# A recurrent loop on one core: two gates share 128 PSUM columns, a gate's rows change order, and the seeds move

## The chip, the cores and the metric

The kernel runs on one core of one Trainium2 chip. The metric is device time in microseconds (us) of one execution. The engines are TensorE (PE in the profile; its weight loads are PEld), VectorE (DVE), ScalarE (ACT), GpSimd (POOL) and SyncE (SP), which issues DMAs. Each engine works through its own list of instructions in order and waits where an operand isn't ready. SBUF is the on-chip memory, PSUM the memory that TensorE writes into.

## The reference

The input x has 4 sequences of 512 tokens with 512 features; cond has 4 rows of 512. An attention layer (normalised, scaled and shifted by cond, 16 heads) adds its result to x. Then a GRU runs over the 512 tokens with cond as the first state, and after it two causal four-tap convolutions. Each layer adds to x:

```
x = x + attention(x, cond)
x = x + GRU(cond, x)        # scan over the 512 tokens
x = x + conv(x, cond)
x = x + conv(x, cond) + b

def cell(h, x):
    gi = x @ W_ih + b_ih
    gh = h @ W_hh + b_hh
    r = sigmoid(i_r + h_r)
    z = sigmoid(i_z + h_z)
    n = tanh(i_n + r * h_n)
    h_new = (1.0 - z) * n + z * h
```

The GRU is sequential: the state of token t is needed for token t+1. One step multiplies a 4 x 512 state by a 512 x 1536 matrix.

## The kernel before

Before the loop, the kernel loads and splits the weights into a high and a low half-precision part (`Whi`, `Wlo`), computes keys and values of all tokens, and the first block of 32 tokens of attention. The loop over t (line 1180) then does one GRU step per turn. All other work (attention of later blocks, their input products `gi`, the convolutions of earlier blocks) is cut into small tasks. A planner (`Queue`) puts some of them into each step by estimated cost: `q_.head` (line 1196) places work for VectorE, ScalarE and GpSimd, at most 1130, 1900 and 3300 ns each, at the start of the step; `q_.pe` (line 1235) places matmuls of at most 1150 ns (1300 in the first 64 steps) behind the step's own. The order on every engine is the order of the program's text: it is written out by hand.

One step, with the lines:

- `mm` (lines 1198 to 1212) multiplies the state. The state lies on partitions in four chunks k of 128 features. Each product goes to four groups of 32 PSUM partitions (qq) at once, one quarter of the columns each. The state is split too: `A` is its half-precision part, `BT` holds A again and the rest of the state, HS - A, in slots of 4 rows (one row per sequence). The tile `X` [128, 256] has gate r in columns 0 to 127 and gate z in 128 to 255, so one matmul has 256 columns: 16 with `Wlo` and A, 16 with `Whi` and BT. The tile `Y` [128, 128] holds gate n: 32 matmuls of 128 columns.
- VectorE turns X by 32 x 32 blocks into `TX` (line 1214), and adds the two row sets into `S` (1216). ScalarE's tanh makes both gates `ZT` (1217). A sigmoid is written as a tanh of half the argument.
- VectorE turns Y into `TY` (1226), with an output order that steps by 4 elements inside runs of 4. A scan (1227) multiplies by r and adds up the parts of n into `N`. ScalarE's tanh goes to `D1` (1228); line 1220 makes (1 - z) in `D0`; line 1229 makes z times the state from `HH`, half the state.
- Two scans (1237, 1238) make the new state as `A` (half precision) and `HS` (full). `prep` (1104 to 1111) fills BT from them: VectorE the difference (1108), ScalarE the copies (1109) and HH (1110). GpSimd keeps the state for the output in `hsb` (1242).
- PSUM is not cleared: ScalarE writes the input part of the next step, the seed, into X (`seedX`, 1099, behind ZT) and Y (`seedY`, 1102, behind the tanh), and the matmuls add to it. Seeds come from `G`, filled every four steps by `load_g` (1070 to 1074), eight DMAs on SyncE's queue. The first two steps are seeded by matmuls (`seed_first`, 1083).
- GpSimd also does small work of the planner: a chain of 15 operations per block that makes reciprocal roots (lines 257 to 272, 407, 409), a small product per head (443), and parts of the convolutions (1122 to 1124, 1146). VectorE's work of the planner is mostly the row maximum of a head (442) and the convolution's taps (1133, 1137).

## Time and profile before

| what | value |
|---|---|
| median of 3 runs | 1899.21 us (1896.22 to 1905.69) |
| the profiled execution | 1898.34 us, its span 1896.6 us |
| granted TensorE clock, mean | 0.984 |
| busy: PE, PEld | 1633.8 us (86%), 1162.2 us (61%) |
| busy: DVE, ACT, POOL | 1453.0 us (77%), 1176.5 us (62%), 329.0 us (17%) |
| the loop | from 229 to 1876 us of the span |

The span is from the first to the last instruction. Busy time is the sum of an engine's instructions; matmuls overlap in TensorE's pipeline, so its share says little by itself. In a group line the columns are: line, engine, operation, output <- inputs, shapes, count, then busy us and mean ns of one, then the idle time before them and what ended it. In a timeline line they are start, length (us), engine, line, operation; "x16" means that 16 instructions are merged.

### The profile page before, as it was taken

What the parts mean: (1) busy time and instruction counts of PE and PEld (TensorE: products, weight loads), DVE (VectorE), ACT (ScalarE), POOL (GpSimd) and SP (SyncE); (2) the same over time, 40 slices, a digit from 0 to 9 for tenths busy, and PEclk for the clock granted to TensorE, in tenths of its full rate; (3) what the DMA queues carried; (4) which work ended last, traced back from release to release, by engine and by line L of the source; (5) the groups of instructions that cost most, each with busy time, mean ns of one, the idle gap of its engine ahead of it and who ended that gap; (6) DMA issues with size and microseconds to landing.
All of it is one profiled execution on the core that took longest, in us unless ns stands there. A gap on an engine that the chain in (4) does not pass through costs nothing. (4 is left out here: it accounts for less than half of the span.)

```text
span 1896.6 us, 113881 instructions
## 1 busy us (share of the span) xinstructions
PE 1633.8 (86%) x48944; PEld 1162.2 (61%) x48944; DVE 1453.0 (77%) x5315; ACT 1176.5 (62%) x4578; POOL 329.0 (17%) x1151
## 2 busy tenths in 40 slices
PE   5789899988899999999898989999898989987553
PEld 2444567666666666666666666666666666666442
DVE  4786477877888787878787887878787878887675
ACT  4544475766677666767575766666575757664442
POOL 1361011202111212111111111111111111111111
PEclk9999999999999999999999999999999999999998
DMA  5652011010100101010101011010101000001000
GB/s 187 221 186 112 24 51 35 22 43 19 29 24 16 34 19 54 13 39 11 38 14 31 20 35 38 21 31 11 40 13 39 12 26 19 23 24 27 16 17 9
DMA packets 68919, 78.09 MB, mean 41 GB/s; under 512 B 6560, under 2 KB 54720, under 8 KB 67776
## 3 DMA queue, kind: packets, MB, share of 16 engines
q1 hardware_dynamic: 68416, 70.82, 12.1%
q8 instruction: 384, 6.29, 1.4%
q14 instruction: 119, 0.97, 0.2%
HBM read 44.58 MB, written 26.21 MB: 37 GB/s over the span
## 5 line engine op out<-in xcount | busy, mean ns | idle before, releaser
L1200 PEld LDWEIGHTS <-BT 128*8 128x8 f16 (+1 forms) x24576 | 449.7, 89 | 69.4 <-issue 4.4
L1200 PE MATMUL X<-Wlo,A 128*4 128x256 f16 x8192 | 313.2, 273 | 187.8 <-DVE A L1237 145.4
L1217 ACT ACTIVATE ZT<-S 128x32 f32<-128x32 f32 x512 | 134.6, 263 | 503.0 <-DVE S L1216 503.0
L1214 DVE STREAM_TRANSPOSE TX<-X 128x256 f32<-128x256 f32 x512 | 228.7, 447 | 146.6 <-PE X L1200 146.3
L1242 POOL TENSOR_SCALAR hsb<-HS 128x16 f32<-128x16 f32 x512 | 115.0, 225 | 1241.5 <-DVE HS L1238 1221.4
L1200 PEld LDWEIGHTS <-A 128*4 128x4 f16 x8192 | 151.2, 83 | 282.7 <-DVE A L1237 260.1
L1200 PE MATMUL X<-Whi,BT 128*8 128x256 f16 x8192 | 315.3, 274 | 0.2 <-issue 0.2
L1200 PE MATMUL Y<-Whi,BT 128*16 128x128 f16 x8192 | 206.3, 220 | 1.5 <-issue 1.4
L1226 DVE STREAM_TRANSPOSE TY<-Y 128x128 f32<-128x128 f32 x512 | 204.8, 400 | 3.3 <-PE Y L1200 2.1
L1200 PE MATMUL Y<-Wlo,BT 128*16 128x128 f16 x8192 | 205.3, 220 | 0.8 <-issue 0.8
L1099 ACT ACTIVATE X<-G 128x256 f32<-128x256 f32 x510 | 202.1, 396 | 2.9 <-DMA G<-GD 1.4
L451 ACT ACTIVATE PX<-ps,nb,rqs 128x512 f32<-128x512 f32 x256 | 195.4, 763 | 10.8 <-DVE nb L443 5.8
L1227 DVE TENSOR_TENSOR_SCAN N<-ZT,TY 128x64 f32<-128x64 f32 x512 | 154.1, 301 | 54.8 <-ACT D L1220 1.8
L1237 DVE TENSOR_TENSOR_SCAN A<-D,D 128x32 f16<-128x32 f32 x512 | 115.3, 225 | 94.7 <-ACT D L1228 94.2
L442 DVE TENSOR_REDUCE mx<-ps 128x1 f32<-128x512 f32 x256 | 175.0, 684 | 11.4 <-PE ps L435 11.1
L297 PE MATMUL ptp<-ident,PX 128*128 128x128 f32 x1024 | 170.0, 288 | 1.3 <-DVE gs L570 0.6
L1109 ACT ACTIVATE BT<-A 128x64 f16<-128x64 f16 x512 | 131.0, 256 | 52.8 <-DVE A L1237 2.0
L297 PEld LDWEIGHTS ptp<-ident,PX 128*128 128x128 f32 x1024 | 110.4, 142 | 78.0 <-issue 61.6
L471 ACT ACTIVATE PT<-ptp 128x512 f32<-128x512 f32 x248 | 143.3, 584 | 12.8 <-PE ptp L297 12.7
L1102 ACT ACTIVATE Y<-G 128x128 f32<-128x128 f32 x510 | 141.2, 277 | 0.5 <-issue 0.3
L479 PEld LDWEIGHTS po<-V,PT 128*32 128x32 f32 x8192 | 95.3, 111 | 57.9 <-issue 53.4
L1216 DVE TENSOR_TENSOR S<-TX 128x32 f32<-128x32 f32 x512 | 114.8, 224 | 17.5
(257 smaller groups left out, 2754.9 us busy)
## 6 DMA issues: line engine op xcount, KB each, us to landing
GD<-gs SPq DMA_DIRECT2D x45, 256.0 KB
G<-GD SPq DMA_DIRECT2D x512, 16.0 KB
G<-GD SPq DMA_DIRECT2D x512, 8.0 KB
xp<-in_x_dram SPq DMA_DIRECT2D x16, 256.0 KB
xb<-in_x_dram SPq DMA_DIRECT2D x16, 256.0 KB
xhl<-XD SPq DMA_DIRECT2D x32, 128.0 KB
out_dram<-ob SPq DMA_DIRECT2D x16, 256.0 KB
wst<-in_L_cond_W_qkv_dram SPq DMA_DIRECT2D x6, 512.0 KB
```

Source lines behind the costliest of these rows:

```text
L297: nc.tensor.transpose(dst[:, 128 * j:128 * j + 128], src[:, 128 * j:128 * j + 128], ident)
L442: nc.vector.tensor_reduce(s["mx"][:, h:h + 1], s[("s", j, q)], AX.X, ALU.max)
L451: nc.scalar.activation(pe_, s[("s", j, q)], AF.Exp, bias=s["nb"][:, h:h + 1], scale=s["rqs"][:, h:h + 1], accum_out=s["ls"][:, h:h + 1])
L471: nc.scalar.activation(pt_, s[("pt", h)], AF.Copy)
L1099: nc.scalar.activation(X.rearrange("p (g c) -> p g c", g=2), G[(t // 4) % 2][:, t % 4, 0:2, :], AF.Copy)
L1102: nc.scalar.activation(Y, G[(t // 4) % 2][:, t % 4, 2, :], AF.Copy)
L1109: nc.scalar.activation(Bt[:, :, 1:8:2, :], A[:, :, 1].rearrange("p (k b) -> p k b", k=4).unsqueeze(2).to_broadcast([P, 4, 4, 4]), AF.Copy)
L1200: nc.tensor.matmul(dst[32 * qq:32 * qq + M, :], lhs, W[:, k, cols].rearrange("p g (j q s) -> p q g j s", j=4, q=4)[:, qq], start=False, st ...
L1214: nc.vector.transpose(TX.rearrange("p a r -> p (a r)"), X)
L1217: nc.scalar.activation(zt[:, :, :, 2], S.rearrange("p (g a) -> p g a", g=2), AF.Tanh, scale=0.5 * IWS)
L1226: nc.vector.transpose(TY.rearrange("p h j b k -> p j h k b"), Y.rearrange("p (j h k b) -> p j h k b", j=4, h=2, k=4))
L1227: nc.vector.tensor_tensor_scan(f(NN), f(zt[:, 0]), TY[:, 0].rearrange("p j b k -> p (j b k)"), 0.0, ALU.mult, ALU.add)
```

## The change

- X is 128 columns wide. Gates r and z use the same columns and differ by row: of 16 rows in each group of 32, the first 8 are r, the next 8 z. The matmuls of a step for X become 64 of 128 columns, in four sets: r low with A, z low with A (two zero slots ahead of it, 12 rows), r high with A and HS - A, z high with both behind two zero slots (16 rows).
- BT keeps only X's operands. Y's operands lie in a new tile `BY`, in the row order (sequence, part), filled by two GpSimd operations in `prep`. TY's output order then has runs of 16 elements.
- S, ZT, G, `load_g` (12 DMAs), `seed_first` and the constants follow the new rows.
- seedX moves behind the tanh of n, seedY behind `prep`.
- HH goes: the tanh of n and z times the state are made with the opposite sign, and the state's scans subtract.

```
-            nc.tensor.matmul(X, zz[:, 0:128], zz[:, 0:256], start=True, stop=True, skip_group_check=True)
+            nc.tensor.matmul(Xb, zz[:, 0:128], zz[:, 0:256], start=True, stop=True, skip_group_check=True)
...
     def load_g(c):
         for qq in range(4):
-            nc.sync.dma_start(g[32 * qq + 4:32 * qq + 8, :, 0:2, :], GD[i][qq, :, t0_:t0_ + 4, 0:2, :])
-            nc.sync.dma_start(g[32 * qq + 8:32 * qq + 12, :, 2, :], GD[i][qq, :, t0_:t0_ + 4, 2, :])
+            nc.sync.dma_start(g[32 * qq:32 * qq + 4, :, 0, :], GD[i][qq, :, t0_:t0_ + 4, 0, :])
+            nc.sync.dma_start(g[32 * qq + 8:32 * qq + 12, :, 0, :], GD[i][qq, :, t0_:t0_ + 4, 1, :])
+            nc.sync.dma_start(g[32 * qq + 2:32 * qq + 18:4, :, 1, :], GD[i][qq, :, t0_:t0_ + 4, 2, :])
...
     def seedX(t):
-        nc.scalar.activation(X.rearrange("p (g c) -> p g c", g=2), G[(t // 4) % 2][:, t % 4, 0:2, :], AF.Copy)
+        nc.scalar.activation(X, G[(t // 4) % 2][:, t % 4, 0, :], AF.Copy)
...
     def prep(A, HS, t):
-        nc.vector.tensor_tensor(Bt[:, :, 0:4:2, :], dup(HS[:, :, 1]), dup(A[:, :, 1]), ALU.subtract)
-        nc.scalar.activation(Bt[:, :, 1:8:2, :], A[:, :, 1].rearrange("p (k b) -> p k b", k=4).unsqueeze(2).to_broadcast([P, 4, 4, 4]), AF.Copy)
-        nc.scalar.activation(HH, HS[:, :, 1], AF.Copy, scale=0.5)
+        h4, a4 = (v[:, :, 1].rearrange("p (k b) -> p k b", k=4) for v in (HS, A))
+        nc.vector.tensor_tensor(Bt[:, :, 3], h4, a4, ALU.subtract)
+        nc.scalar.activation(Bt[:, :, 2], a4, AF.Copy)
+        two = lambda v: v[:, :, 1].unsqueeze(2).to_broadcast([P, 16, 2])
+        nc.gpsimd.tensor_tensor(By[:, 1, :, 1:3], two(HS), two(A), ALU.subtract)
+        nc.gpsimd.tensor_scalar(By[:, :, :, 0:4:3], A[:, :, 1].unsqueeze(1).unsqueeze(3).to_broadcast([P, 2, 16, 2]), 1.0, 1.0, ALU.mult, ALU.mult)
...
             for k in range(4):
-                mm(X, A[:, 4 * k:4 * k + 4, 1], 4, Wlo, k, slice(0, 2))
+                mm(X, A[:, 4 * k:4 * k + 4, 1], 4, Wlo, k, slice(0, 1))
             for k in range(4):
-                mm(X, Bt[:, k, 0:2, :].rearrange("p s b -> p (s b)"), 8, Whi, k, slice(0, 2))
+                mm(X, st(k, 0, 3), 12, Wlo, k, slice(1, 2))
+            for k in range(4):
+                mm(X, st(k, 2, 4), 8, Whi, k, slice(0, 1))
+            for k in range(4):
+                mm(X, st(k, 0, 4), 16, Whi, k, slice(1, 2))
...
-                mm(Y, Bt[:, k, 4:8].rearrange("p s b -> p (s b)"), 16, Wlo, k, slice(2, 3))
+                mm(Y, By[:, 0, 4 * k:4 * k + 4].rearrange("p b s -> p (b s)"), 16, Wlo, k, slice(2, 3))
...
-                mm(Y, Bt[:, k, 0:4].rearrange("p s b -> p (s b)"), 16, Whi, k, slice(2, 3))
+                mm(Y, By[:, 1, 4 * k:4 * k + 4].rearrange("p b s -> p (b s)"), 16, Whi, k, slice(2, 3))
-            TX = wk.tile([P, 8, 32], F32, name="TX", tag="TX", bufs=1)
+            TX = wk.tile([P, 4, 32], F32, name="TX", tag="TX", bufs=1)
...
-            nc.vector.tensor_tensor(S.rearrange("p (a b) -> p a b", a=8), TX[:, :, 0:4], TX[:, :, 4:8], ALU.add)
-            nc.scalar.activation(zt[:, :, :, 2], S.rearrange("p (g a) -> p g a", g=2), AF.Tanh, scale=0.5 * IWS)
-            if 1 < t + 1 < T:
-                seedX(t + 1)
+            tx = TX[:, :, 0:16].rearrange("p j (g s b) -> p g s j b", g=2, s=2)
+            nc.vector.tensor_tensor(S, tx[:, :, 0], tx[:, :, 1], ALU.add)
+            nc.scalar.activation(zt[:, :, :, 2], S.rearrange("p g j b -> p g (j b)"), AF.Tanh, scale=0.5 * IWS)
...
-            nc.vector.transpose(TY.rearrange("p h j b k -> p j h k b"), Y.rearrange("p (j h k b) -> p j h k b", j=4, h=2, k=4))
+            nc.vector.transpose(TY.rearrange("p h j b k -> p j h (b k)"), Y.rearrange("p (j h r) -> p j h r", j=4, h=2))
...
-            nc.scalar.activation(D1[:, :, 0], NN[:, :, 3], AF.Tanh, scale=0.5 * IWS)
-            nc.vector.scalar_tensor_tensor(D1[:, :, 1], zt[:, 1, :, 2], 1.0, HH, ALU.add, ALU.mult)
+            nc.scalar.activation(D1[:, :, 0], NN[:, :, 3], AF.Tanh, scale=-0.5 * IWS)
+            nc.vector.scalar_tensor_tensor(D1[:, :, 1], d0[:, :, 1], 1.0, HS[:, :, 1], ALU.subtract, ALU.mult)
             if 1 < t + 1 < T:
-                seedY(t + 1)
+                seedX(t + 1)
...
-            nc.vector.tensor_tensor_scan(f(An), f(d0), f(D1), 0.0, ALU.mult, ALU.add)
-            nc.vector.tensor_tensor_scan(f(HSn), f(d0), f(D1), 0.0, ALU.mult, ALU.add)
+            nc.vector.tensor_tensor_scan(f(An), f(d0), f(D1), 0.0, ALU.mult, ALU.subtract)
+            nc.vector.tensor_tensor_scan(f(HSn), f(d0), f(D1), 0.0, ALU.mult, ALU.subtract)
             if t + 1 < T:
-                Bt, HH = prep(A, HS, t + 1)
+                Bt, By = prep(A, HS, t + 1)
+                if t > 0:
+                    seedY(t + 1)
```

In `seed_first` the step's rows are cleared by four matmuls of zeros first, and r and z are added by two matmuls per group, as X's rows are shared.

More of the change, by code (lines that the diff above doesn't have):

```diff
@@ L170, in body @@
     pb = ctx.enter_context(tc.tile_pool(name="pb", bufs=1, space=PS))
-    X = pg.tile([P, 256], F32, name="X")
+    Xb = pg.tile([P, 256], F32, name="X")
+    X = Xb[:, 0:128]
     NN = pg.tile([P, 16, 4], F32, name="N")
@@ L188, in body @@
     brow = cst.tile([P, 1], F32, name="brow")
-    nc.vector.tensor_reduce(brow, ident.rearrange("p (q s) -> p q s", q=4)[:, :, 4:8], AX.XY, ALU.add)
+    nc.vector.tensor_reduce(brow, ident.rearrange("p (q b s) -> p q b s", q=4, b=8)[:, :, 0:4, 1], AX.XY, ALU.add)
     rows = cst.tile([34, P], F32, name="rows")
@@ L224, in body @@
     D0 = [cst.tile([P, 16, 2], F32, name=f"D0{i}") for i in range(2)]
-    BT = [cst.tile([P, 4, 8, 4], F16, name=f"BT{i}") for i in range(2)]
+    BT = [cst.tile([P, 4, 4, 4], F16, name=f"BT{i}") for i in range(2)]
+    BY = [cst.tile([P, 2, 16, 4], F16, name=f"BY{i}") for i in range(2)]
     for i in range(2):
@@ L230, in body @@
         nc.gpsimd.memset(BT[i], 0.0)
+        nc.gpsimd.memset(BY[i], 0.0)
     nc.gpsimd.memset(zz, 0.0)
@@ L1042, in scan_constants @@
             nc.gpsimd.memset(g, 0.0)
-            nc.gpsimd.tensor_scalar(g[:, :, 2, :], bhn.unsqueeze(1).to_broadcast([P, 4, P]), 1.0, 1.0, ALU.mult, ALU.mult)
+            nc.gpsimd.tensor_scalar(g[:, :, 1, :], bhn.unsqueeze(1).to_broadcast([P, 4, P]), 1.0, 1.0, ALU.mult, ALU.mult)
         for tl_ in (x2b[1], x3b[1]):
             nc.gpsimd.memset(tl_, 0.0)
-        for v, m in ((sel, 1), (selY, 2)):
+        for v, c in ((sel, slice(0, 4)), (selz, slice(8, 12)), (selY, slice(2, 16, 4))):
             nc.gpsimd.memset(v, 0.0)
-            nc.gpsimd.tensor_scalar(v[:, :, 4 * m:4 * m + 4], ident.rearrange("p (b t) -> p t b", b=4)[:, 0:2, :], 1.0, 1.0,
-                                    ALU.mult, ALU.mult)
-    sel, selY = lt("sel", [P, 2, 8]), lt("selY", [P, 2, 12])
-    G = [lt(f"G{i}", [P, 4, 3, P]) for i in range(2)]
+            nc.gpsimd.tensor_scalar(v[:, :, c], ident.rearrange("p (b t) -> p t b", b=4)[:, 0:2, :], 1.0, 1.0, ALU.mult, ALU.mult)
+    sel, selz, selY = lt("sel", [P, 2, 4]), lt("selz", [P, 2, 12]), lt("selY", [P, 2, 16])
+    G = [lt(f"G{i}", [P, 4, 2, P]) for i in range(2)]
     x2b = [lt(f"x2b{i}", [P, 16, 35]) for i in range(2)]
@@ L1086, in seed_first @@
             r = 32 * qq
-            for g, n in enumerate("rz"):
-                nc.tensor.matmul(X[r:r + 8, 128 * g:128 * g + 128], sel[:, t],
-                                 gs0[n][:, qq, :], start=(g == 0), stop=True, skip_group_check=True)
+            nc.tensor.matmul(X[r:r + 32, :], zz[:, 0:32], zz[:, 0:128], start=True, stop=True, skip_group_check=True)
+        for qq in range(4 - 4 * y):
+            r = 32 * qq
+            nc.tensor.matmul(X[r:r + 4, :], sel[:, t], gs0["r"][:, qq, :], start=False, stop=True, skip_group_check=True)
+            nc.tensor.matmul(X[r:r + 12, :], selz[:, t], gs0["z"][:, qq, :], start=False, stop=True, skip_group_check=True)
         for qq in range(4 * y):
@@ L1094, in seed_first @@
             r = 32 * qq
-            nc.tensor.matmul(Y[r:r + 12, :], selY[:, t], gs0["n"][:, qq, :], start=False, stop=True,
+            nc.tensor.matmul(Y[r:r + 16, :], selY[:, t], gs0["n"][:, qq, :], start=False, stop=True,
                              skip_group_check=True)
     def seedX(t):
-        nc.scalar.activation(X.rearrange("p (g c) -> p g c", g=2), G[(t // 4) % 2][:, t % 4, 0:2, :], AF.Copy)
+        nc.scalar.activation(X, G[(t // 4) % 2][:, t % 4, 0, :], AF.Copy)
     def seedY(t):
-        nc.scalar.activation(Y, G[(t // 4) % 2][:, t % 4, 2, :], AF.Copy)
+        nc.scalar.activation(Y, G[(t // 4) % 2][:, t % 4, 1, :], AF.Copy)
     def prep(A, HS, t):
-        Bt = BT[t % 2]
-        HH = wk.tile([P, 16], F32, name="HH", tag="HH")
-        nc.vector.tensor_tensor(Bt[:, :, 0:4:2, :], dup(HS[:, :, 1]), dup(A[:, :, 1]), ALU.subtract)
-        nc.scalar.activation(Bt[:, :, 1:8:2, :], A[:, :, 1].rearrange("p (k b) -> p k b", k=4).unsqueeze(2).to_broadcast([P, 4, 4, 4]), AF.Copy)
-        nc.scalar.activation(HH, HS[:, :, 1], AF.Copy, scale=0.5)
-        return Bt, HH
+        Bt, By = BT[t % 2], BY[t % 2]
+        h4, a4 = (v[:, :, 1].rearrange("p (k b) -> p k b", k=4) for v in (HS, A))
[4 more added lines that the diff above has]
+        nc.gpsimd.tensor_scalar(By[:, :, :, 0:4:3], A[:, :, 1].unsqueeze(1).unsqueeze(3).to_broadcast([P, 2, 16, 2]), 1.0, 1.0, ALU.mult, ALU.mult)
+        return Bt, By
     HSB = {}
@@ L1177, in body @@
         seed_first(0, 0)
-        Bt, HH = prep(A, HS, 0)
+        Bt, By = prep(A, HS, 0)
         due = None
@@ L1201, in mm, with st @@
                                      skip_group_check=True)
+            def st(k, s0, s1):
+                return Bt[:, k, s0:s1].rearrange("p s b -> p (s b)")
             for k in range(4):
-                mm(X, A[:, 4 * k:4 * k + 4, 1], 4, Wlo, k, slice(0, 2))
+                mm(X, A[:, 4 * k:4 * k + 4, 1], 4, Wlo, k, slice(0, 1))
             for k in range(4):
-                mm(X, Bt[:, k, 0:2, :].rearrange("p s b -> p (s b)"), 8, Whi, k, slice(0, 2))
+                mm(X, st(k, 0, 3), 12, Wlo, k, slice(1, 2))
[3 more added lines that the diff above has]
+                mm(X, st(k, 0, 4), 16, Whi, k, slice(1, 2))
             if t == 0:
@@ L1209, in body @@
             for k in range(4):
-                mm(Y, Bt[:, k, 4:8].rearrange("p s b -> p (s b)"), 16, Wlo, k, slice(2, 3))
+                mm(Y, By[:, 0, 4 * k:4 * k + 4].rearrange("p b s -> p (b s)"), 16, Wlo, k, slice(2, 3))
             for k in range(4):
-                mm(Y, Bt[:, k, 0:4].rearrange("p s b -> p (s b)"), 16, Whi, k, slice(2, 3))
-            TX = wk.tile([P, 8, 32], F32, name="TX", tag="TX", bufs=1)
+                mm(Y, By[:, 1, 4 * k:4 * k + 4].rearrange("p b s -> p (b s)"), 16, Whi, k, slice(2, 3))
+            TX = wk.tile([P, 4, 32], F32, name="TX", tag="TX", bufs=1)
             nc.vector.transpose(TX.rearrange("p a r -> p (a r)"), X)
-            S = wk.tile([P, 64], F32, name="S", tag="S", bufs=1)[:, 0:32]
-            nc.vector.tensor_tensor(S.rearrange("p (a b) -> p a b", a=8), TX[:, :, 0:4], TX[:, :, 4:8], ALU.add)
-            nc.scalar.activation(zt[:, :, :, 2], S.rearrange("p (g a) -> p g a", g=2), AF.Tanh, scale=0.5 * IWS)
-            if 1 < t + 1 < T:
-                seedX(t + 1)
+            S = wk.tile([P, 2, 4, 4], F32, name="S", tag="S", bufs=1)
+            tx = TX[:, :, 0:16].rearrange("p j (g s b) -> p g s j b", g=2, s=2)
+            nc.vector.tensor_tensor(S, tx[:, :, 0], tx[:, :, 1], ALU.add)
+            nc.scalar.activation(zt[:, :, :, 2], S.rearrange("p g j b -> p g (j b)"), AF.Tanh, scale=0.5 * IWS)
             nc.scalar.activation(d0[:, :, 1], zt[:, 1, :, 2], AF.Copy, scale=-0.5, bias=0.5)
```

## The prediction

> **What bounds the kernel now.** I read the cores view first (one core, granted clock 0.984, and 1.00 over the loop, so no clock argument), then the page's slices (TensorE and VectorE both high all along), then the timeline of single steps. The loop of 512 steps runs from 229 to 1876 us of a span of 1896.6 us: 3.22 us a step. This is one step near the end, where little other work is queued (start us, length us, engine, line, operation, tiles):

> ```profile
> 1865.11 0.22 DVE L1237 TENSOR_TENSOR_SCAN A<-D,D 128x32 f16<-128x32 f32 x1 [0.18 <-ACT D L1228]
> ...
> 1865.37 0.26 ACT L1109 ACTIVATE BT<-A 128x64 f16<-128x64 f16 x1
> ...
> 1865.39 0.61 PE L1200 MATMUL X<-Wlo,A 128*4 128x256 f16 x16 [1.25 <-ACT Y L1102]
> 1865.48 0.19 DVE L1108 TENSOR_TENSOR BT<-HS,A 128x32 f16<-128x32 f32 x1
> ...
> 1865.53 0.23 POOL L1242 TENSOR_SCALAR hsb<-HS 128x16 f32<-128x16 f32 x1 [2.78 <-DVE HS L1238]
> ...
> 1865.82 0.61 PE L1200 MATMUL X<-Whi,BT 128*8 128x256 f16 x16
> 1866.26 0.40 PE L1200 MATMUL Y<-Wlo,BT 128*16 128x128 f16 x16
> 1866.48 0.40 PE L1200 MATMUL Y<-Whi,BT 128*16 128x128 f16 x16
> 1866.48 0.45 DVE L1214 STREAM_TRANSPOSE TX<-X 128x256 f32<-128x256 f32 x1 [0.81 <-PE X L1200]
> ...
> 1866.97 0.19 DVE L1216 TENSOR_TENSOR S<-TX 128x32 f32<-128x32 f32 x1
> 1867.08 0.40 DVE L1226 STREAM_TRANSPOSE TY<-Y 128x128 f32<-128x128 f32 x1
> 1867.19 0.26 ACT L1217 ACTIVATE ZT<-S 128x32 f32<-128x32 f32 x1 [1.47 <-DVE S L1216]
> ...
> 1867.58 0.30 DVE L1227 TENSOR_TENSOR_SCAN N<-ZT,TY 128x64 f32<-128x64 f32 x1
> ...
> 1867.91 0.19 ACT L1228 ACTIVATE D<-N 128x16 f32<-128x16 f32 x1
> ...
> 1868.13 0.23 DVE L1237 TENSOR_TENSOR_SCAN A<-D,D 128x32 f16<-128x32 f32 x1 [0.18 <-ACT D L1228]
> ```

> See a closed ring. Counted from the end of scan A ("E"): X matmuls start at E+54 ns and end 1045 later; 53 to TX; TX 447; 34 to S; 612 from S to scan N; 333 to the tanh; 220 to scan A; 224 for it: 3.02 us. N waits for TY (S+109, 400 long, 103 after it), not for the tanh ZT, which ends at S+487.

> ```profile
> ACT ZT L1217 <- DVE S L1216: 503.0, 497, 7.3
> ...
> DVE TX L1214 <- PE X L1200: 146.3, 310, 4.3
> ```

> These are two rows of the waits view (who waited for whom: us in total, times, longest): ScalarE idles about a microsecond per step, and VectorE waits for X in 310 steps. From the start times of all 512 steps: in 185 steps TX starts late because VectorE still does other work (47 us in all), in 63 TensorE still does other work when A is ready (24 us), and S is stretched by 16 us. These sit on top of 512 x 3.02.

> **The change, part by part.** Durations are of this profiled execution: 1898.34 us, 1896.6 span and 1.7 around it; the median of three is 0.9 above.

> *TX, 256 to 128 columns.* The same form, 128 plain columns out of PSUM, is in the trace, beside two GpSimd rows used below:

> ```profile
> L393 DVE STREAM_TRANSPOSE rt<-pr 128x128 f32<-128x128 f32 x16 | 4.9, 308 | 0.0
> ...
> L1122 POOL TENSOR_SCALAR x2b<-x2b 128x48 f32<-128x48 f32 x16 | 3.9, 244 | 0.0
> L1124 POOL TENSOR_TENSOR x2b<-x,hsb 128x512 f32<-128x512 f32 x16 | 20.4, 1272 | 0.0
> ```

> 447 to 308: 139 less, all on the ring.

> *TY.* Now 32 runs of 4 elements out: 400. New: 8 runs of 16. Ends 308 (L393, one run) and 400 (no help). I share the 92 by runs: 308 + 92 x 7/31 = 329. N then starts at S+109+329+103 = 541 instead of 612: 71 less. Below 520 it cannot come, as ZT ends at 487 and the shortest hop to N seen is 33.

> *X matmuls.* 32 of 256 columns become 64 of 128. Spacing per 16: 436 for 256 columns, 224 for the Y groups of 128. X end: 3 x 224 + 397 = 1069 against 1045: 24 more. The second group (z, low weights) needs ScalarE's copy of A (L1109), now 16 elements: between 202 (L1110's 16 elements) and 256 (the old 64), begun at E+34, with 54 to TensorE: ready at E+290 to 344; the first group covers to E+278. So 12 to 66 of wait; I take 20, nearer the 16-element row. VectorE's subtraction (L1108, 32 elements in 192, now 16) is done by E+340, needed at E+520: free with 180 of cover. A step: 139 + 71 - 44 = 166 ns, times 511: **85 us less**.

> [...]

> *VectorE-late steps.* X ends 44 later and the subtraction some 20 earlier, so of each of the 185 late steps up to 64 is taken back: **11 us less**.

> *TensorE's other work.* It runs between the last Y matmul and the next A. That window shrinks by 166 + 44 = 210. Moving each step's own end by that puts 205 steps in wait instead of 63, 50 us instead of 24, and 4 more in VectorE-late steps: **30 us more** (20 to 40: a filler that itself waits may move along).

> *Y's stationary moves to GpSimd.* Two operations per step after HS, ahead of hsb: a subtraction over 32 elements, a copy over 64. GpSimd starts 83 after HS ends, E+200. Nearest rows: 222 for 16 elements (L261), 244 for 48, 377 for 128 (L1146), independent ones 198 apart: the pair ends near E+720. With 50 of hop it is due at E+920, since Y starts at E+970. Cover 200. The low end is E+641. The high end: 300 apart as in the chain below, the first behind the running subtraction (142), the second behind one VectorE tap (345), ending E+1277, 357 late. I take 0 late, as all three nearest rows are short and hsb, which overlaps L1108 in every step, shows 225. The trace has the reverse: S took 1266 instead of 192 when L1124 had begun 60 to 90 earlier. [...]

> What is queued on GpSimd ahead of the pair counts too. In 14 blocks a chain of 15 small operations (lines 257 to 409) holds it:

> ```profile
> 617.36 0.23 POOL L1242 TENSOR_SCALAR hsb<-HS 128x16 f32<-128x16 f32 x1 [2.80 <-DVE HS L1238]
> 618.02 0.20 POOL L257 TENSOR_SCALAR nw_v<-rv 128x16 f32<-128x16 f32 x1 [0.44 <-DVE rv L394]
> ...
> 622.30 0.20 POOL L409 TENSOR_SCALAR nrq<-rq 128x16 f32<-128x16 f32 x1
> 622.59 0.22 POOL L1242 TENSOR_SCALAR hsb<-HS 128x16 f32<-128x16 f32 x1
> ```

> See hsb begin 2.0 us late; nobody minds, but the pair will stand there, and Y with it. Mean lateness 2.05, plus 0.17 as the next step comes sooner, less the cover 0.20: 2.0 x 14: **28 us more**.

> *Seeds.* seedX (396) leaves the place behind ZT; TN is bound by N (33 behind it), so this frees nothing. Behind the tanh, at 128 columns like seedY's 277, it ends at tanh+360 and X may start at tanh+498: cover 84 after the hop; gone, the rest is paid one for one. seedY, behind the copy of A, ends near E+500, due E+920. The copy L1109, behind seedX on ScalarE, starts after A anyway, 120 past seedX's end.

> *Scan signs, HH.* L1229 now waits for D0, which ends 130 earlier than it did; 181 of idle behind L1229 covers it. HH's 202 on ScalarE was hidden by the 503 us of idle.

> *SyncE.* Each load of G is 12 issues, not 8, some 350 apart: 2.86 to 4.3 us, three steps ahead of use. At block changes only about one step remains: first issue to first seed 6.85 us, eight issues spanning 4.2 to 6.2, and seeds that waited did so under 2.1 after the last issue. With 1.43 added and seeds 0.2 later, eleven of 15 wait 0.2 to 1.4: **8 us more** (0, if the spans stay; 15, if they grow by half).

> *Before the loop:* two small GpSimd operations, eight matmuls, four issues: 0, between -1 and +2.

> Sum: -85 - 11 + 30 + 28 + 8 = -30: 1868 for this execution, **1869** on the median.

> **Rivals.** *GpSimd becomes the bound (slower).* The pair ends past E+920 in ordinary steps; every 100 costs 51 us. Break-even is 59 late, a pair of 780 instead of 520. At a pair of 860, 140 late: 1869 + 72 = 1941. For: it is new on the ring, two kinds of blocking are possible. Against: rows under 250. *TY stays at 400:* 36 back, 8 of it never spent on collisions: 1897, no change. For: 128 elements, same source. *The fillers eat it:* budgets of 1150 and 1130 per step stay, so TensorE's wait grows to 84 instead of 54: 1899. *Better:* TY at 308, no wait for the copy, seeds' loads hidden, collisions 5 less: 21 x 0.51 + 20 x 0.51 + 8 + 5: 34 off, 1835; typically 1843.

> **How the numbers follow.** Forecast 0.48 (own range 1850 to 1888), GpSimd-bound 0.20, better 0.15, TY unhelped 0.10, eaten 0.07. About 0.5% (9.5 us) is what a measurement can tell. Faster 0.46 + 0.15 + 0.02; same 0.02 + 0.06 + 0.05 + 0.02; slower 0.18 + 0.02 + 0.02. Range 1837 to 1912: half of the GpSimd case and the tail of the good one are left out, and of the bounds only the far end of the pair.

> **What would show it.** L1214 near 308 and L1226 near 329 with N 541 after S; 64 X matmuls in about 1.09 us; quiet steps at 2.86; in 14 steps Y's first matmul about 2 us late behind GpSimd; more TensorE waits for its own fillers. Wrong it would be if Y's matmuls wait for GpSimd in ordinary steps, if VectorE's taps behind the pair stretch past X, or if X waits for seedX.

## The result and the profile after

The changed kernel takes 2155.86 us (median of 4 runs, 2151.89 to 2161.02); the kernel before, on the same chip, 1897.72 (4 runs, 1892.54 to 1905.69). The ratio on record is 1.1343, with a 95% interval of 1.1313 to 1.1374 (the two medians alone divide to 1.136): 258 us slower, where 29 us faster was forecast. The profiled execution took 2161.02 us, 2159.2 of it span. Its granted clock is 0.970 (0.984 before), and 0.98 in the loop (1.00 before), so the clock is not where 13% went.

A quiet step of the changed kernel, to be held against the one shown of before (timeline; start us, length us, engine, line, operation, tiles, idle time before and what ended it):

```profile
2112.16 0.22 DVE L1251 TENSOR_TENSOR_SCAN A<-D,D 128x32 f16<-128x32 f32 x1 [0.23 <-ACT D L1242]
...
2112.44 0.40 PE L1208 MATMUL X<-Wlo,A 128*4 128x128 f16 x16 [1.14 <-DVE A L1251]
...
2112.68 0.25 POOL L1117 TENSOR_TENSOR BY<-HS,A 128x32 f16<-128x32 f32 x1 [2.41 <-DVE HS L1252]
...
2112.89 0.27 POOL L1118 TENSOR_SCALAR BY<-A 128x64 f16<-128x64 f16 x1
2112.91 0.62 PE L1208 MATMUL X<-Whi,BT 128*8 128x128 f16 x32
...
2113.36 0.40 PE L1208 MATMUL Y<-Wlo,BY 128*16 128x128 f16 x16
...
2113.65 0.32 DVE L1229 STREAM_TRANSPOSE TX<-X 128x128 f32<-128x128 f32 x1 [0.94 <-PE X L1208]
...
2114.57 0.30 DVE L1241 TENSOR_TENSOR_SCAN N<-ZT,TY 128x64 f32<-128x64 f32 x1
...
2114.90 0.18 ACT L1242 ACTIVATE D<-N 128x16 f32<-128x16 f32 x1
2115.17 0.22 DVE L1251 TENSOR_TENSOR_SCAN A<-D,D 128x32 f16<-128x32 f32 x1 [0.21 <-ACT D L1242]
```

From scan A to scan A it is 3.01 us: even this step gained next to nothing, where 2.86 us was expected. Two hops have grown: TX starts 0.12 us after X's end at 2113.53 (0.05 before), and scan A 0.09 us after the end of the tanh (0.03 before). GpSimd's pair is done at 2113.16 and Y's matmuls follow those of X at once.

But few steps look like this. Over all steps, the 5th percentile of the length is 2974 ns (3018 before), the mean 3724 (3222 before). What fills the difference stands in the waits view (who waited for whom: us in all, times, longest), where TensorE waits for "issue", that is, for nothing that the profile shows:

```profile
ACT ZT L1233 <- DVE S L1232: 647.3, 500, 7.3
DVE TX L1229 <- PE X L1208: 367.4, 415, 4.5
PEld L1208 <- issue: 206.5, 277, 2.4
...
PEld po L482 <- issue: 109.0, 285, 2.4
PE X L1208 <- issue: 93.1, 153, 1.3
...
PE Y L1208 <- issue: 59.7, 85, 2.3
```

Before, the same row for the loop's weight loads was:

```profile
PEld L1200 <- issue: 4.9, 14, 1.2
```

Here TensorE stops in the middle of a run of equal matmuls whose operands are all there (TensorE's timeline):

```profile
375.35 0.41 PE L1208 MATMUL X<-Wlo,A 128*4 128x128 f16 x16
375.57 0.40 PE L1208 MATMUL X<-Wlo,BT 128*12 128x128 f16 x15
377.05 0.22 PE L1208 MATMUL X<-Wlo,BT 128*12 128x128 f16 x1 [1.07 <-issue]
377.05 0.66 PE L1208 MATMUL X<-Whi,BT 128*8 128x128 f16 x32
```

Fifteen of sixteen go, the last comes 1.2 us late. Counting starts of neighbours in one group that are over 400 ns apart, there are 302 such stalls (279 us of gaps) against 11 (7.7 us) before, from 229 us on. In a run of them the stalls stand behind 2511, 2639, 2767, 2895, 3023 and 3151 matmuls: always 128 apart. Of the 301 distances from stall to stall, 283 are whole multiples of 128 matmuls, and 15 more are one off. 128 matmuls with their weight loads are 256 instructions, and that is what one packet of the queue called "instruction" holds. The queue's row (packets, MB, share), of after and then of before:

```profile
q8 instruction: 510, 8.36, 1.6%
```

```profile
q8 instruction: 384, 6.29, 1.4%
```

All these packets are of 16,384 bytes. 384 x 256 = 98,304 against 97,888 TensorE instructions before; 510 x 256 = 130,560 against 130,672 after: at 64 bytes each, the queue carries TensorE's program. Before, the spacing of packets in the loop is 3.43 us at the 5th percentile, 4.07 at the median and 6.22 at the 95th, and the closest two are 3.23 apart; after, 3.41, 3.76 and 4.59, the closest 3.25. The closest are no closer; the wide spacings are gone. And a stall ends 1.24 to 1.58 us (5th to 95th percentile) after a packet has landed: a tight delay, as if the stalled instruction had been in that packet.

The trace can be counted to show that it was. Take, just before the end of each stall, the number of instructions that TensorE has started (all its rows of the trace, semaphore instructions too) and the number of packets that have landed. In 300 of the 302 stalls the first is 256 times the second plus 193, to the instruction; so it is in 243 of 245 stalls of the run with 32 tiny matmuls below. And in all 14 kernels, with n packets landed, TensorE is never past instruction 256 n + 449 (449 is 193 + 256): the instruction behind that mark never starts sooner than 1.11 us after the next packet has landed. So each stall is TensorE at the end of what has been delivered. After, it starts the instruction behind the mark within 1.7 us of the landing at 423 of 495 packets of the loop; before, at 73 of 369.

So the reading is: **TensorE's program arrived, in these runs, at no more than one packet in about 3.4 us** (the 5th percentile: 3.43 before, 3.41 after), 13 ns an instruction. That it came no faster when TensorE waited for it shows in the changed kernel, which waits for nearly every packet and still gets them 3.76 us apart in the median; what sets the spacing is not shown. TensorE used it up faster: 16 matmuls and their loads go in 223 ns, 7 ns an instruction. A step has about 184 TensorE instructions before (128 of the recurrence, the rest of other work) and 64 more after: 32 matmuls and their weight loads. 248 / 256 x 3.41 = 3.3 us is then the estimated least for a mean step, and at the median spacing it is 3.64. With 184 it is 2.45 and 2.70, under the ring's 3.02.

### The profile page after: what moved, and what is told of

The parts are those of the page before. It is cut to its first block, busy times and chain, and to the rows that moved or that the text cites. A ratio compares the mean times of both kernels' runs of the same rounds, so it can differ in the third digit from the quotient of the medians.

```text
span 2159.2 us, 147948 instructions
## 1 busy us (share of the span) xinstructions
PE 1728.4 (80%) x65336; PEld 1276.7 (59%) x65336; DVE 1368.7 (63%) x5315; ACT 1098.9 (51%) x4066; POOL 550.5 (25%) x2179
## 3 DMA queue, kind: packets, MB, share of 16 engines
q14 instruction: 133, 1.09, 0.2%
## 5 line engine op out<-in xcount | busy, mean ns | idle before, releaser
L1117 POOL TENSOR_TENSOR BY<-HS,A 128x32 f16<-128x32 f32 x512 | 136.3, 266 | 1388.9 <-DVE HS L1252 1321.3
L1208 PEld LDWEIGHTS <-BT 128*12 128x12 f16 (+2 forms) x24576 | 374.9, 89 | 109.2 <-issue 97.7
L1229 DVE STREAM_TRANSPOSE TX<-X 128x128 f32<-128x128 f32 x512 | 162.0, 316 | 385.9 <-PE X L1208 367.4
L1208 PE MATMUL X<-Whi,BT 128*8 128x128 f16 (+1 forms) x16384 | 352.8, 222 | 54.9 <-issue 53.6
L1208 PE MATMUL X<-Wlo,A 128*4 128x128 f16 x8192 | 215.8, 221 | 137.6 <-DVE A L1251 79.4
L1208 PEld LDWEIGHTS <-BY 128*16 128x16 f16 x16384 | 267.4, 91 | 97.1 <-issue 77.8
L1208 PE MATMUL Y<-Wlo,BY 128*16 128x128 f16 x8192 | 228.3, 222 | 45.6 <-issue 30.7
L1208 PE MATMUL Y<-Whi,BY 128*16 128x128 f16 x8192 | 225.3, 222 | 29.4 <-issue 29.0
L1208 PE MATMUL X<-Wlo,BT 128*12 128x128 f16 x8192 | 218.8, 222 | 22.7 <-issue 21.5
L482 PE MATMUL po<-V,PT 128*32 128x32 f32 x8192 | 137.8, 202 | 49.5 <-issue 49.4
L1242 ACT ACTIVATE D<-N 128x16 f32<-128x16 f32 x512 | 94.8, 185 | 157.7 <-DVE N L1241 119.2
```

The source lines that it names most:

```text
L482: nc.tensor.matmul(s["po"][32 * b:32 * b + 32, 32 * h:32 * h + 32], s["PT"][h][:, kt, 32 * b:32 * b + 32], V[:, 4 * b + kt, 32 * h:32 * h ...
L1117: nc.gpsimd.tensor_tensor(By[:, 1, :, 1:3], two(HS), two(A), ALU.subtract)
L1208: nc.tensor.matmul(dst[32 * qq:32 * qq + M, :], lhs, W[:, k, cols].rearrange("p g (j q s) -> p q g j s", j=4, q=4)[:, qq], start=False, st ...
L1229: nc.vector.transpose(TX.rearrange("p a r -> p (a r)"), X)
```

## Experiments

Rivals to it: that the 64 narrow matmuls cost time on the array; that GpSimd is the bound, as the prediction's slow case had it; that the seeds or the twelve loads stall. A quiet step is the 5th percentile of the step length throughout. "Stalls" are gaps over 400 ns inside a group of equal matmuls.

**X back to 256 columns, all else as changed.** The second group of columns of X is left to itself, so z is computed from its seed alone.

```
-                mm(X, A[:, 4 * k:4 * k + 4, 1], 4, Wlo, k, slice(0, 1))
-            for k in range(4):
-                mm(X, st(k, 0, 3), 12, Wlo, k, slice(1, 2))
-            for k in range(4):
-                mm(X, st(k, 2, 4), 8, Whi, k, slice(0, 1))
-            for k in range(4):
-                mm(X, st(k, 0, 4), 16, Whi, k, slice(1, 2))
+                mm(Xb, A[:, 4 * k:4 * k + 4, 1], 4, Wlo, k, slice(0, 2))
+            for k in range(4):
+                mm(Xb, st(k, 2, 4), 8, Whi, k, slice(0, 2))
```

> The changed kernel, but X's products are again 32 matmuls of 256 columns per step instead of 64 of 128; gate z's columns are then not read (VectorE still turns 128 columns), so gate z is computed from its seed alone: that part is left out. All else of the change stays, GpSimd's pair, the seeds, the 12 loads. Theory (TensorE's instruction stream: 248 instead of 184 TensorE instructions per step, and the stalls stand every 128 matmuls): back to 184 per step, so the time falls to 1870 to 1900 us, with few stalls inside a group of matmuls. [...]

Measured: 1914.96 us (6 runs), ratio 1.0085 (1.0061 to 1.0109). 241 of the 258 us are gone with 32 matmuls a step, though they cover the same columns. Not all of the 241 is stalls: the quiet step is 49 ns shorter as well (2925 against 2974), 25 us over the loop. Stalls: 31 (23 us). The rest of the change alone still is 15 us slower than before, and above the range that was expected. GpSimd's pair, the moved seeds and the twelve loads are all in this kernel, so none of them is the 241 us.

**The kernel before with 16 or 32 tiny matmuls a step.** They are 4 x 4, on zeros, behind the filler of each step (`range(16)` or `range(32)`).

```
+            for u in range(32):
+                r = 32 * (u % 4)
+                nc.tensor.matmul(idle[r:r + 4, 0:4], zz[:, 0:4], zz[:, 0:4], start=False, stop=True, skip_group_check=True)
```

> The kernel before, plus 16 tiny matmuls of 4 columns behind the step's other TensorE work (zeros added to an unused part of PSUM). 216 TensorE instructions per step. Theory (instruction stream, at best 256 per 3.4 us): 2.9 us a step is below the 3.2 used, so little, 1910 to 1960 us. Rival (TensorE's time, about 10 ns a matmul, 0.16 us a step): 1915 us.

> The kernel before, plus 32 such tiny matmuls: 248 TensorE instructions per step, as many as the changed kernel. Theory: at least 3.3 us a step plus uneven stalls, 2050 to 2200 us, with stalls every 128 matmuls. Rival (TensorE's time, 0.32 us a step, most of it in the window before the next state): 1950 us, as the run with two wide matmuls.

Measured: 1990.32 us with 16 (2 runs, ratio 1.0478, 1.0456 to 1.05), a miss to the slow side; 2156.96 with 32 (2 runs, 1.1355, 1.1302 to 1.1408), the time of the changed kernel within 1 us, with none of its edits. That it agrees so closely is luck: its quiet step is 155 ns longer (the probe has a fault, below), and its stalls are fewer. The 16 were expected at 3.4 us a packet, 2.9 us a step; at the 3.76 of the changed kernel 216 instructions take an estimated 3.17 us, more than the ring, and that fits the miss. Of the 32's kernel, the instruction queue and three rows of the waits view:

```profile
q8 instruction: 512, 8.39, 1.7%
```

```profile
PEld L1239 <- issue: 152.3, 330, 1.2
PEld L1200 <- issue: 110.1, 164, 1.9
PE Y L1239 <- ACT Y L1102: 108.2, 206, 1.9
```

Line 1239 is the tiny matmuls. The second row is the wait for issue. The third is a fault of the probe: the spare columns that the added matmuls write share a tile with Y, so they also wait for Y's seed. Part of the first row looks to come of the same fault: the control below, which has it too, has 134.5 us in that row and 4 stalls. With 32 of them behind that wait the quiet step is 111 ns longer, some 57 us in all. The stalls, 207 us of gaps between equal matmuls, don't rest on these rows.

**The same place, two wide matmuls instead.** A control: time on the array, but 4 more instructions a step, not 32 or 64.

```
+            for u in range(2):
+                nc.tensor.matmul(idle[:, 0:384], zz[:, 0:128], zz[:, 0:384], start=False, stop=True, skip_group_check=True)
```

> The kernel before, plus two matmuls of 384 columns behind the step's other TensorE work: about the TensorE time of 32 tiny ones (0.32 us), but only 4 more instructions. Theory and rival agree here: 1940 to 1960 us. It is the control for the run with 32 tiny matmuls.

Measured: 2042.79 us (2 runs, 1.0754, 1.0732 to 1.0775), a miss by 80 us. Its waits view (the probe is line 1238) says why:

```profile
PEld L1200 <- DVE BT L1108: 157.1, 496, 0.3
PEld L1238 <- issue: 134.5, 283, 0.8
PE Y L1238 <- ACT Y L1102: 128.6, 245, 1.7
```

The wide ones also wait for Y's seed, and are then still running when A is ready: X starts 376 ns after A even in quiet steps, 54 before. So the control costs time, but in another way, and the step lengths keep the two apart (ns; TensorE instructions and packets of the whole program):

| kernel | instructions | packets | quiet step | mean step | mean less quiet | stalls | us |
|---|---|---|---|---|---|---|---|
| before | 97,888 | 384 | 3018 | 3222 | 204 | 11 | 1898 |
| two wide | 99,936 | 392 | 3343 | 3489 | 146 | 4 | 2043 |
| X of 256 columns | 97,904 | 384 | 2925 | 3243 | 318 | 31 | 1915 |
| 16 tiny | 114,272 | 448 | 3028 | 3392 | 364 | 132 | 1990 |
| 32 tiny | 130,656 | 512 | 3129 | 3710 | 581 | 245 | 2157 |
| changed | 130,672 | 510 | 2974 | 3724 | 750 | 302 | 2156 |

The wide control makes every step longer and hardly ever stalls (4 times, 3.2 us). The 16 tiny ones hardly lengthen a quiet step (10 ns) and stall in others; the 32 do both. Stalls go with the number of TensorE's instructions, not with what these compute.

**The changed kernel with fewer instructions elsewhere.** Three of four products of probabilities and values are left out from the third block of attention on.

```
+                if kt and i > 1:
+                    return
...
-                                     start=(kt == 0), stop=(kt == 3), skip_group_check=True)
+                                     start=(kt == 0), stop=(kt == 3 or i > 1), skip_group_check=True)
```

> The changed kernel with its narrow X, but from the third block of attention on three of four products of probabilities and values are left out (the sum over keys has one quarter of them). The planner's order stays; TensorE's instructions fall from 130,672 to about 119,900. Theory (instruction stream): the two runs with tiny matmuls lie at 114,272 and 1990 us, 130,656 and 2157 us, so on that line 2048 us, 2030 to 2070. Rival (GpSimd's pair or the new hops bound the changed kernel): 2140 to 2160 us, since these products lie beside the ring.

Measured: 1998.08 us (2 runs, 1.0529, 1.0467 to 1.0591), below what either theory gave. The narrow X is all there; 468 packets, 130 stalls (90 us).

```profile
PEld L1210 <- issue: 105.5, 214, 2.2
```

42 packets less took 158 us off, 3.8 us each, which is the median spacing; but the left-out products also free the array, so the size is not pure. That the 64 narrow matmuls by themselves cost what was lost is out: they run as in the changed kernel, with the same quiet step (2974), and 158 us of it are gone.

**The seed of X moved, in the kernel before.** Now to the two grown hops.

```
-            if 1 < t + 1 < T:
-                seedX(t + 1)
...
+                seedX(t + 1)
                 seedY(t + 1)
```

> The kernel before, with one part of the change: seedX goes behind the tanh of n, ahead of seedY. Theory (in the old place VectorE's wait for the tanh covers seedX; in the new one TX needs a wait of its own, an extra semaphore instruction): TX starts 120 instead of 53 ns after X's matmuls, and X starts some 30 late since seedX of 256 columns takes 396; a quiet step 3.12 instead of 3.02 us, 1930 to 1950 us. Rival (the 120 comes from the 128 columns of X): TX stays at 53, 1905 to 1915 us.

Measured: 1930.94 us (1.0153, 1.0123 to 1.0183), as expected. In its timeline X ends at 1905.80 and TX starts 0.12 later, against 0.05 before:

```profile
1905.19 0.61 PE L1200 MATMUL X<-Whi,BT 128*8 128x256 f16 x16
...
1905.92 0.45 DVE L1214 STREAM_TRANSPOSE TX<-X 128x256 f32<-128x256 f32 x1 [0.89 <-PE X L1200]
```

Before, seedX came ahead of the tanh on ScalarE's list; VectorE's wait for that tanh covered it as well. Moved behind the tanh, it is not covered, and TX must wait for TensorE and ScalarE both: VectorE's list gets one more semaphore instruction, and TX starts 68 later in a quiet step. X starts 16 later too; the quiet step is 3104, 86 more than before.

**The saved state read from A, in the kernel before.** GpSimd then reads A, as it does in the changed kernel.

```
-            nc.gpsimd.tensor_scalar(HSB[i].rearrange("p (a t) -> p a t", t=32)[:, :, t % 32], HS[:, :, 1], 1.0, 1.0,
+            nc.gpsimd.tensor_scalar(HSB[i].rearrange("p (a t) -> p a t", t=32)[:, :, t % 32], A[:, :, 1], 1.0, 1.0,
```

> The kernel before, with GpSimd's hsb taken from A instead of HS, so that GpSimd reads A (the state is then kept in half precision). Theory (scan A, which overwrites an older A, must then wait for GpSimd too): scan A starts 88 instead of 33 ns after the tanh, a quiet step 3.08 us, 1918 to 1930 us. Rival (the 88 comes from the seeds or the sign): no change, 1899 us.

Measured: 1921.9 us (1.01, 1.0077 to 1.0124), as expected. The next writer of that buffer, a scan A, now also has to know that GpSimd is done. GpSimd was done long before, but the wait for it takes a place. VectorE has one semaphore instruction ahead of scan A in both kernels. Before, it waits for VectorE's own work and the scan itself for the tanh; now it waits for the tanh, and the scan for GpSimd. So the tanh's end has to pass through two instructions: in one step, the first ends 45 ns after the tanh and the scan starts 43 later. From the tanh's end to scan A it is 88 ns in the median step, 33 before.

**Twelve loads in place of eight, in the kernel before.**

```
-            nc.sync.dma_start(g[32 * qq + 4:32 * qq + 8, :, 0:2, :], GD[i][qq, :, t0_:t0_ + 4, 0:2, :])
+            for n in range(2):
+                nc.sync.dma_start(g[32 * qq + 4:32 * qq + 8, :, n, :], GD[i][qq, :, t0_:t0_ + 4, n, :])
```

> The kernel before, with the seeds of r and z loaded by a DMA each: 12 issues instead of 8 for each load of G, as in the changed kernel. Theory of the prediction (at block changes the seeds come later, 8 us in all, 0 to 15): 1903 to 1912 us. Rival (hidden): 1899 us.

Measured: 1907.86 us (1.0033, 1.0014 to 1.0051): 6 us more; 8 were forecast.

**X of 256 columns, and GpSimd's chain of 15 cut in four.** As in the first experiment, but the chain's reciprocal root comes in pieces, three operations in a step and then two, three and four in the next ones, each piece a stage of its own in the plan.

```
-                rsqrt(rq, v, 16, ear, nc.gpsimd)
-                rs1()
+                s["gen"] = rsqrt_ops(rq, v, 16, ear, nc.gpsimd)
+                rsp(3)()
...
+        def rsp(n):
+            def f():
+                for _ in range(n):
+                    next(s["gen"], 0)
+                if n == 4:
+                    rs1()
+            return f
```

> The changed kernel with wide X matmuls (as in the run of that name, 1915 us, gate z from its seed alone), and GpSimd's chain of 15 operations split over four steps. Theory (the chain holds up GpSimd's pair, and Y, by 2 us in 14 steps): 1885 to 1895 us. Rival (that lateness lies beside other work): 1915 us.

Measured: 1897.69 us (0.9972, 0.9953 to 0.999), 17 less than without the cut, and just above the 1885 to 1895 that were expected. N comes 59 ns a step sooner in the mean (579 after S, from 638): 30 us, close to the 28 forecast for the chain. About 18 us of that are lost again where X starts late behind TensorE's other work (217 after A in the mean, from 182).

**Y's new row order alone, in the kernel before.** X stays at 256 columns, seedX behind ZT. Three forms. In the first, ScalarE writes the copies into Y's stationary operand, GpSimd doubles VectorE's difference, and the chain is cut as above (the loads, the selection rows and TY's order are as in the change):

```
-        nc.vector.tensor_tensor(Bt[:, :, 0:4:2, :], dup(HS[:, :, 1]), dup(A[:, :, 1]), ALU.subtract)
-        nc.scalar.activation(Bt[:, :, 1:8:2, :], A[:, :, 1].rearrange("p (k b) -> p k b", k=4).unsqueeze(2).to_broadcast([P, 4, 4, 4]), AF.Copy)
+        nc.vector.tensor_tensor(Bt[:, :, 0], h4, a4, ALU.subtract)
+        nc.scalar.activation(Bt[:, :, 1], a4, AF.Copy)
+        nc.scalar.activation(By[:, :, :, 0:4:3], A[:, :, 1].unsqueeze(1).unsqueeze(3).to_broadcast([P, 2, 16, 2]), AF.Copy)
+        nc.gpsimd.tensor_scalar(By[:, 1, :, 1:3].rearrange("p (k b) s -> p k b s", k=4), Bt[:, :, 0].unsqueeze(3).to_broadcast([P, 4, 4, 2]), 1.0, 1.0, ALU.mult, ALU.mult)
...
+            nc.vector.transpose(TY.rearrange("p h j b k -> p j h (b k)"), Y.rearrange("p (j h r) -> p j h r", j=4, h=2))
```

In the second (shown against the first), ScalarE does all of it and the chain is whole:

```
-        nc.gpsimd.tensor_scalar(By[:, 1, :, 1:3].rearrange("p (k b) s -> p k b s", k=4), Bt[:, :, 0].unsqueeze(3).to_broadcast([P, 4, 4, 2]), 1.0, 1.0, ALU.mult, ALU.mult)
+        nc.scalar.activation(By[:, 1, :, 1:3].rearrange("p (k b) s -> p k b s", k=4), Bt[:, :, 0].unsqueeze(3).to_broadcast([P, 4, 4, 2]), AF.Copy)
```

> The kernel before with one part of the change alone, Y's row order: X stays 256 columns, seeds, HH and signs stay. BY is filled by ScalarE (copies of A) and GpSimd (the difference, copied from BT, so that GpSimd does not read A), and the chain is split over four steps. Theory: TY 311 instead of 400, N 523 after S, a quiet step 2.93 us, less what TensorE's other work takes back: 1862 to 1880 us. Rival (any GpSimd work in the ring costs more than it gives): 1900 us or more.

> The kernel before with Y's row order alone, as in the run that filled BY by GpSimd, but ScalarE fills all of BY (a third small copy, of the difference out of BT), and the chain on GpSimd is left as it was. Theory (the row order's gain of 89 ns is real, and was lost there to the wait of VectorE's subtraction for GpSimd and to the split chain): subtraction 34 after HS again, 436 between the X groups, N 523 after S, a quiet step 2.93 us, 1862 to 1880 us. Rival (TensorE's and VectorE's other work take the 89 back): 1890 us or more.

Measured: first form 1929.1 us (1.0136, 1.0111 to 1.0162), a miss; second form **1890.21 us (7 runs, 0.9938, 0.9915 to 0.9961)**: faster than both kernels, by less than was expected. In both, N comes 520 to 522 after S, as hoped. In the first, the old trouble has a new owner. GpSimd now reads BT, so the difference, BT's writer, waits for GpSimd and starts later:

```profile
1896.49 0.23 DVE L1250 TENSOR_TENSOR_SCAN A<-D,D 128x32 f16<-128x32 f32 x1 [0.18 <-ACT D L1241]
...
1896.94 0.18 DVE L1119 TENSOR_TENSOR BT<-HS,A 128x16 f16<-128x16 f32 x1
...
1897.23 0.24 PEld L1213 LDWEIGHTS <-BT 128*8 128x8 f16 x12
1897.26 0.39 PE L1213 MATMUL X<-Whi,BT 128*8 128x256 f16 x8
```

The difference begins 0.22 us after A's end (0.15 in the step shown of before), and X's second group follows its first (at 1896.77) by 0.49 us, 0.43 in the step of before. A quiet step is 2981, and its mean 302 above it; the first form has many late steps (in 1 of 100 the tanh waits 1.85 us behind N). That the cut chain puts the planner's work in another order is a reading of the trace, not tested by itself. The second form has a quiet step of 2933, 85 ns less than before. Over 511 steps that would be 43 us; 12 came through (the kernel before took 1901.88 on that chip). ScalarE's list is the next thing to be late there, as seedX on it waits for its load and holds the tanh behind it:

```profile
L1101 ACT ACTIVATE X<-G 128x256 f32<-128x256 f32 x510 | 201.2, 395 | 13.0 <-DMA G<-GD 11.0 <-PE ptp L299 0.8 <-PE ps L437 0.6
```

The row for seedX of before has 2.9 us of idle, 1.4 of it for the load. The tanh starts 68 after N in the mean, 38 before; X starts 131 after A, 101 before: some 15 us each, so TensorE's other work takes as much as ScalarE's list.

The third form adds the scans' sign to the second and drops HH; seedX stays behind ZT.

```
-            nc.scalar.activation(D1[:, :, 0], NN[:, :, 3], AF.Tanh, scale=0.5 * IWS)
-            nc.vector.scalar_tensor_tensor(D1[:, :, 1], zt[:, 1, :, 2], 1.0, HH, ALU.add, ALU.mult)
+            nc.scalar.activation(D1[:, :, 0], NN[:, :, 3], AF.Tanh, scale=-0.5 * IWS)
+            nc.vector.scalar_tensor_tensor(D1[:, :, 1], d0[:, :, 1], 1.0, HS[:, :, 1], ALU.subtract, ALU.mult)
```

> The run with BY filled by ScalarE, plus one more part of the change: HH goes, the tanh of n and line 1229 change sign and the scans subtract, so ScalarE has one small copy less per step (202 ns). Theory (ScalarE, which now starts ZT late in over a hundred steps, is what took part of the 89 back): ZT waits for S in more steps again, 1870 to 1885 us. Rival (TensorE's other work took it): 1890 us, unchanged.

Measured: 1948.98 us (1.0264, 1.0244 to 1.0283), a miss by over 60. Its timeline:

```profile
1909.59 0.39 ACT L1101 ACTIVATE X<-G 128x256 f32<-128x256 f32 x1
...
1909.92 0.21 ACT L1223 ACTIVATE D<-ZT 128x16 f32<-128x16 f32 x1
1910.08 0.18 ACT L1231 ACTIVATE D<-N 128x16 f32<-128x16 f32 x1
1910.16 0.18 DVE L1232 SCALAR_TENSOR_TENSOR D<-D,HS 128x16 f32<-128x16 f32 x1
...
1910.44 0.23 DVE L1240 TENSOR_TENSOR_SCAN A<-D,D 128x32 f16<-128x32 f32 x1
```

Line 1232 now needs D0 (line 1223), which stands behind seedX's 0.39 us on ScalarE. It ends after the tanh, and scan A starts 0.18 after the tanh instead of 0.03: the quiet step is 3073, 140 above the second form. Nor did one small copy less help ScalarE: the tanh still starts 67 after N in the mean.

## Where the prediction was right and where it was wrong

- **X matmuls: the step that failed.** It costed 32 more matmuls by what the array takes, 224 ns for 16 of 128 columns against 436 for 16 of 256. On the array that held: groups follow each other by 223 to 225 in the median of the changed kernel, and X ends 49 later in a quiet step, where the working had 44. But each one is also two instructions that have to arrive, and the step, which counted the DMAs that every edit issues, did not count these. Their price was most of the 241 us between the changed kernel and the one with X of 256 columns: less the 25 of the longer quiet step, some 216 us that the sum had at nothing. The rows were there to bound it: 384 instruction packets, none closer than 3.23 us, and 184 instructions in a step of 3.22 us. None of the rivals had it, so the range missed as well. The runs do not show the loss as time on the array: 16 matmuls of 128 columns, in four groups of 32 partitions, took 223 ns, and it came as stalls at multiples of 128 matmuls.
- **TX, 308 forecast:** 316 measured. **TY, 329 forecast, N 541 after S:** 311 and 520 to 522. The row order does what it says, and more; N is then bound by ZT, as the working said it would be below 520.
- **Seeds, "this frees nothing" and a cover of 84:** wrong, as the move takes a cover away that was not seen, VectorE's wait for the tanh. TX starts 68 later; done alone, with the 16 on X, the move costs 29 us.
- **Y's stationary on GpSimd:** the pair was sized rightly (due at A's end + 920; forecast 720, near 770 in quiet steps, 266 ns for its first operation). Missed was that GpSimd's reading of A adds a wait ahead of scan A: 55 a step, 20 us when done alone.
- With these two, the quiet step adds up: 3022 less 166 is 2856; less 18 (TY and N), plus 8 (TX), 5 (X), 68 and 55 is 2974; measured 2974. So 44 ns of the 166 were gained on the ring.
- **Scan signs, "181 of idle behind L1229 covers it":** true in the changed kernel only because seedX has moved away from ahead of D0. With seedX in its old place the sign costs 140 a step. The two edits belong together, and the move's 68 is the price of the other.
- **TensorE's other work, 30 more:** with X of 256 columns X starts 81 later after A in the mean (182 against 101), 41 us, part of it the stalls of that run. **VectorE-late steps, 11 less:** TX's lateness above its own quiet hop went from 92 to 46 in the mean there, 24 us less; that a longer hop hides more is a reading, not tested by itself. **Chain, 28 more:** 30 by the cut chain. **Loads, 8 more:** 6.
- **Rivals.** "GpSimd becomes the bound" is out: in the changed kernel TensorE's weight loads wait for it 12 times, 15.8 us in all, and the taps behind the pair are stretched 5 or 6 times by some 70 ns. The long operation of the convolution still stretches S, up to 1.20 us, 10 times. "TY stays at 400" is out by its 311. "The fillers eat it" is partly so, by the 41 us above.

Left open: what sets the spacing of the packets, and why it is 3.76 us in the median where the closest are 3.25. That the stall is a late packet is counted from instructions started and packets landed; no view ties an instruction to its packet. How much of the 158 us in the run with fewer products is late packets and how much is the freed array isn't settled, nor the late steps of the cut chain.

## What to carry to other kernels

Count the instructions that an engine gets in a microsecond, beside the work in them: here 256 TensorE instructions (128 matmuls) in 3.4 to 3.8 us was about the limit, and splitting wide matmuls hit it while the array had time to spare. When an instruction is moved or an engine becomes a reader of a buffer, write down every wait of the next writer or reader anew: a wait for an engine that was long done still cost 55 and 68 ns on the ring, once per step.
